# First FFN and preparation of a batch handed out a unit later in layer 0 of a two-layer macaron transformer

## The chip, the cores and the metric

The kernel runs on one core of one Trainium2 chip. The metric is the device time of one execution in microseconds, lower is better. The kernel before takes 3639.21 us, the median of 3 runs (3634.64 to 3644.63).

## The reference

The input x has 16 batches of 512 tokens with 128 channels. Two layers follow each other; the change lies in layer 0 alone. Cut to what matters:

```python
# layer 0
x = x + 0.5 * L0_ffn(layernorm(x))      # first FFN
x = x + L0_attn(layernorm(x))           # 16 heads of 8, clipped relative positions in scores and context
x = x + 0.5 * L0_ffn(layernorm(x))      # second FFN, same weights
# layer 1
x = x + 0.5 * L1_ffn(x)                 # attention over the batch axis, layer norm, mixture of 8 experts
x = x + L1_attn(x)                      # causal linear attention, relu features
x = x + 0.5 * L1_ffn(x)

def L0_ffn(x):                          # inputs and weights quantized to FP4 and back, blocks of 16
    h = silu(q(x) @ q(w_gate).T) * (q(x) @ q(w_up).T)   # 128 -> 352
    return q(h) @ q(w_down).T                           # 352 -> 128
```

## The kernel before

**Units.** Layer 0 (`layer0`) works on half batches. Unit u = 2b + h is half h (256 query rows) of batch b, 32 units in all. Each unit has these steps, and each is a Python generator that yields after a few instructions:

- `head(b,h)`: the first FFN of a half batch (`FFN.half`): statistics of the layer norm on VectorE (L55, L56), quantization on VectorE and GpSimd (L70 to L81), transposes and matmuls on TensorE, and the addition into x (L140). It begins with `xload(b)`, which takes one of five buffers of the tile x and issues the load on SP's queue (L475).
- `prep(b)`: the preparation of a whole batch for attention (`Attn0.prep`): layer norm, transposes, the q and k projections (L286), a split into two float16 parts (L143, L307), and 22 DMA stores on SP's queue to scratch tensors in DRAM: QM (L300), QS and KSd (L302), and rows of QS (L309). `prepV` makes the values.
- `loads(u)`: the loads of that scratch data on SP's queue: the keys KS (L315, once per batch), the queries BD (L329) and TQ (L330). BD and TQ have three buffers, KS two.
- `mxs(b,half)`: the row maxima of the scores. TensorE makes 32 score tiles (L263, and L267 near the diagonal) in three PSUM banks, VectorE takes each one's maxima (L341), and their negatives go through a small DRAM tensor MD (L353) back into a row of BD (L355).
- `main`: the same 32 score tiles again, now with the maxima in BD; ScalarE exponentiates each (L369), TensorE multiplies by the values and the relative table (L272, L274), ScalarE copies out (L403, L412), and the relative part goes through DRAM (L406, L409).
- `fin`: normalizes the context, output projection, addition into x (L443).
- `tail(b,h)`: the second FFN of the half, with `FFN.half` again, and the store of the result (L486).

The two FFNs share one set of work buffers (pool fk, two of each), and nearly all small matmuls and transposes share two PSUM banks (tag mps).

**Order.** A prologue runs some steps one after the other; everything else is put into a list S as (generator, number of steps, from, to), with from and to in units, and `interleave` hands out the step with the smallest place next. So a step that is listed from 3.9 to 5.0 is traced in equal portions over that stretch. The maxima run as one stream over all units, 33 steps each, and `loads(u+1)` is called at the 17th step of the maxima of unit u. By these places the loads of unit v are called at v - 1.94 and its maxima begin at v - 1.42.

The order in which the steps are handed out is not the order on the engines: it gives each instruction its rank. A planner then simulates the kernel with costs of its own and lets each engine take, among the instructions that are ready, the one handed out first. On the chip every engine and SP's queue keep the order that came out of this.

**The lines around the change** are the prologue (three x loads, first FFNs of batches 0, 1 and 2, preparation of batches 0 and 1, the maxima of unit 0 and 14 steps of those of unit 1), the table W with the places, and the constants pl and hl, which tell how many batches ahead the preparation and the first FFN are listed.

Of the kernel before, what the change touches and what calls it, by code (L numbers as in the profile page):

```python
# [141 lines left out]
def f16split(nc, src, hi, lo, eng_lo):  # L142
    nc.vector.tensor_copy(hi,src)  # L143
    eng_lo.tensor_tensor(lo,src,hi,ALU.subtract)

class Attn0:

    def __init__(a, s, wk, pp, wqkv, bqkv, wout, bout, rek, rev):
# [27 lines left out]
        OFF=a.OFF=168  # L176
        W=EW+32
        ekt=wk.tile([8,129],F32,name="ekt")
        with nc.allow_non_contiguous_dma(reason="small"):
            nc.sync.dma_start(ekt,rek.rearrange("r d -> d r"))  # L180
        nc.vector.tensor_tensor(ekt[:,1:],ekt[:,1:],ekt[:,0:1].to_broadcast([8,128]),ALU.subtract)
        pad=wk.tile([8,W],F32,name="pad")
        lo=OFF+24-64
        nc.vector.memset(pad[:,0:lo+1],0.0)
        nc.vector.tensor_copy(pad[:,lo+1:lo+129],ekt[:,1:129])
        nc.vector.tensor_copy(pad[:,lo+129:],ekt[:,128:129].to_broadcast([8,W-lo-129]))
        ph=wk.tile([8,W],F16,name="ph"); pl=wk.tile([8,W],F16,name="pl")
        f16split(nc,pad,ph,pl,nc.vector)
        padk=dr.tile([24,W],F16,name="padk")
        nc.sync.dma_start(padk[0:8],ph); nc.sync.dma_start(padk[8:16],ph); nc.sync.dma_start(padk[16:24],pl)  # L190
# [255 lines left out]
def interleave(*gens):  # L446

    live=[[g,n,0,f,t] for g,n,f,t in (q if len(q)==4 else (*q,0,1) for q in gens)]
    while live:
        k=min(live,key=lambda r:r[3]+(r[4]-r[3])*r[2]/r[1])  # L450
        try: next(k[0]); k[2]+=1
        except StopIteration: live.remove(k)
# [4 lines left out]
def layer0(tc, s, w, src, dst, nb=16):  # L457
    nc=tc.nc
    tok=lambda x,b: x[b].rearrange("(t p) d -> p t d",p=128)
    P="L0_attn_"; names=["W_qkv","b_qkv","W_out","b_out","rel_emb_k","rel_emb_v"]  # L460
    with ExitStack() as c:
        s.const=c.enter_context(tc.tile_pool(name="c",bufs=1))
        pM=c.enter_context(tc.tile_pool(name="pM",bufs=2,space=PS))
        pF=c.enter_context(tc.tile_pool(name="pF",bufs=0,space=PS)) if 0 else pM
        pS=c.enter_context(tc.tile_pool(name="pS",bufs=3,space=PS))
        pX=pS
        pA=c.enter_context(tc.tile_pool(name="pA",bufs=1,space=PS))
        wk=c.enter_context(tc.tile_pool(name="wk",bufs=1))
        fk=c.enter_context(tc.tile_pool(name="fk",bufs=2))
        xk=c.enter_context(tc.tile_pool(name="xk",bufs=5))  # L470
        X={}
        def xload(b):
            if b in X or b>=nb: return
            t=xk.tile([128,4,128],F32,name="x"); X[b]=t
            nc.sync.dma_start(t,tok(src,b))  # L475
        def head(b,h):

            if b<nb: xload(b); yield from F.half(X[b],h,fk,pF)
        def prep(b):
            if b<nb: yield from A.prep(b,X[b],wk,pM)  # L480
        def prepV(b):
            if b<nb: yield from A.prepV(b,pM)
        def tail(b,h):
            if b<0: return
            yield from F.half(X[b],h,fk,pF)
            nc.sync.dma_start(tok(dst,b)[:,2*h:2*h+2,:],X[b][:,2*h:2*h+2,:])  # L486
        def mxs(b,half):
            if b>=nb: return
            yield from A.maxima(b,half,wk,pX,pM)
        def loads(u):  # L490
            if u<2*nb:
                if u%2==0: A.loadK(u//2)
                A.load(u//2,u%2)
        def stream():
            for u in range(1,2*nb):
                for k,_ in enumerate(mxs(u//2,u%2)):
                    if k==16: loads(u+1)
                    yield
        st=stream()
        def part(n):  # L500
            for _ in range(n):
                if next(st,0)==0: return
                yield
        pl,hl=2,3
        W=dict(part=0,V=(.6,.7),fin=(.45,.9),prep=(0,.7),tail=1.0,head=(-.1,1))
        with tc.tile_pool(name="wp",bufs=1) as wp:
            for b in range(3): xload(b)
            F=FFN(s,w["L0_ffn_w_gate"],w["L0_ffn_w_up"],w["L0_ffn_w_down"],wp,pF)
            ffn2=lambda f,b: interleave((f(b,0),21,0,.8),(f(b,1),21,.2,1))
            ffn2(head,0)  # L510
            A=Attn0(s,wp,pS,*[w[P+n] for n in names])
            def run(g):
                for _ in g: pass
            run(prep(0)); run(prepV(0)); loads(0); run(mxs(0,0))
            FFN1.pre(s,wp,[pA.tile([128,512],F32,name=f"av{z}") for z in range(2)]+[pA.tile([128,512],F32,name="rps")],w)
        big=c.enter_context(tc.tile_pool(name="big",bufs=3))
        loads(1); ffn2(head,1); run(prep(1)); run(part(14)); ffn2(head,2)
        S=[(part(99999),33*2*nb,W['part'],2*nb+W['part'])]
        for b in range(nb):
            for h in range(2):  # L520
                u=2*b+h
                def at(g,n,f,t): S.append((g,n,u+f,u+t))
                at(A.main(b,h,X,wk,big,pS,pA,pM),59,0,1)
                fn,tl=(W['fin'],W['tail']) if u<2*nb-2 else ((.3,.5),.6)
                at(A.fin(b,h,X,wk,pM),5,1+fn[0],1+fn[1])
                at(tail(b,h),21,1+fn[1]+.001,1+fn[1]+tl)
                if b+hl<nb: at(head(b+hl,h),21,*W['head'])
                if h==0 and b+pl<nb: at(prep(b+pl),11,*W['prep'])
                if h==1 and b+1<nb: at(prepV(b+1),1,*W['V'])
        interleave(*S)  # L530
# [479 lines left out]
def run_stages(ctx, tc, w, out):  # L1010
    s = K(ctx, tc)
    X2 = s.dram.tile([16, 512, 128], F32, name="X2")
    layer0(tc, s, w, w["L0_attn_x"], X2)
    layer1(tc, s, w, X2, out)
# [23 lines left out]
```

## Time and profile before

| | |
|---|---|
| median of 3 runs | 3639.21 us (3634.64 to 3644.63) |
| the profiled execution | 3633.94 us, its span 3632.2 us |
| mean granted TensorE clock of the profiled execution | 0.90 |
| TensorE matmuls busy | 2825.0 us (78%) |
| VectorE busy | 2444.9 us (67%) |
| ScalarE busy | 1693.8 us (47%) |
| GpSimd busy | 838.9 us (23%) |
| last store of layer 0's result issued (L486) | 2044.9 us |
| statistics of x waiting for its load (L55) | 45.5 us in 11 times |

All durations come from one execution recorded by the hardware profiler, counted from its first instruction. Engines: PE is TensorE, PEld its weight loads, DVE VectorE, ACT ScalarE, POOL GpSimd, SP SyncE, which only issues DMAs here; "SPq" is SP's queue. A row of the timeline has start, duration, engine, line and operation, the tile written and the tiles read, the number of instructions merged, and in brackets the idle time of the engine before it and what ended it. A row of the waits has who waited for whom, the sum in us, how many times, and the longest. A row of the windows has the stretch, its length, and busy time and instruction count of each engine, then the granted clock, the share of the DMA engines' time and GB/s.

### The profile page before, as it was taken

How to read it: one execution, taken by the hardware profiler on the slowest of the kernel's cores; microseconds unless marked ns; L12 is line 12 of the kernel's file. 1: busy time of each engine (PE TensorE's matmuls, PEld its weight loads, DVE VectorE, ACT ScalarE, POOL GpSimd, SP SyncE). 2: the span in 40 equal slices, each digit the busy share in tenths (PEclk: the TensorE clock that was granted, in tenths of full speed). 3: DMA queues.
4: the chain of work that ended last, by engine and by line, in shares of the span. 5: the costliest groups of instructions: out<-in, count | busy, mean ns of one | idle time of the engine just before them, and what ended most of it. 6: DMA issues, size and time to landing. Idle time of an engine off the chain costs nothing. (4 is left out here: it accounts for less than half of the span.)

```text
span 3632.2 us, 95259 instructions
## 1 busy us (share of the span) xinstructions
PE 2825.0 (78%) x40077; PEld 2032.3 (56%) x40077; DVE 2444.9 (67%) x6508; ACT 1693.8 (47%) x3391; POOL 838.9 (23%) x789
## 2 busy tenths in 40 slices
PE   5578989889898889888896388873788888878570
PEld 3357777667676677666775244431565555555230
DVE  5568788777887788877773467774546655655356
ACT  3145555545455454545554155533455454445242
POOL 4122222222222222222110222212112211111226
PEclk8799999999999999999998599886899989989785
DMA  3232222321223222222210111104312222121401
GB/s 105 54 91 71 57 53 59 81 63 52 65 65 77 64 50 58 76 74 62 53 33 19 32 33 36 36 33 123 90 54 73 59 63 56 36 62 36 126 17 46
DMA packets 290159, 217.23 MB, mean 60 GB/s; under 512 B 77402, under 2 KB 257476, under 8 KB 289604
## 3 DMA queue, kind: packets, MB, share of 16 engines
q1 hardware_dynamic: 284468, 207.72, 21.6%
q8 instruction: 315, 5.16, 0.6%
q10 hardware_dynamic: 5264, 3.43, 0.4%
q14 instruction: 112, 0.92, 0.1%
HBM read 110.28 MB, written 100.78 MB: 58 GB/s over the span
## 5 line engine op out<-in xcount | busy, mean ns | idle before, releaser
L341 DVE TRANSPOSE_TENSOR_REDUCE mx<-sps 128x16 f32<-128x512 f32 x1024 | 702.5, 701 | 261.7 <-PE sps L263 137.2
L263 PE MATMUL sps<-a_BD,a_KS 128*128 128x128 f16 x8192 | 736.4, 222 | 136.2 <-DVE mx L341 65.6
L369 ACT ACTIVATE PT<-sps 128x512 f32<-128x512 f32 x1024 | 576.4, 599 | 433.8 <-PE sps L267 238.1
L263 PEld LDWEIGHTS <-a_KS 128*128 128x128 f16 x8192 | 546.1, 98 | 296.4 <-issue 260.0
L59 POOL TENSOR_TENSOR ln_rs<-ln_ve,negh 128x4 f32<-128x4 f32 (+1 forms) x192 | 176.9, 930 | 855.1 <-DVE ln_ve L58 760.6
L267 PE MATMUL sps<-a_TQ,a_ET 128*128 128x64 f16 x7168 | 370.3, 195 | 0.0
L721 DVE SCALAR_TENSOR_TENSOR moe<-mps,oh,moe 128x128 f32<-128x128 f32 x896 | 289.8, 341 | 110.7 <-PE mps L719 96.5
L79 POOL TENSOR_TENSOR q_M<-q_y,q_M 128x704 f32<-128x704 f32 (+2 forms) x129 | 157.0, 1218 | 784.6 <-DVE q_y L78 658.6
L719 PE MATMUL mps<-f_W,T 128*128 128x512 f32 x512 | 297.1, 701 | 24.8 <-DVE moe L721 20.0
L267 PEld LDWEIGHTS <-a_ET 128*128 128x128 f16 x7168 | 311.2, 99 | 2.3 <-issue 1.9
L274 PE MATMUL av<-PT,a_V 128*32 128x256 f32 x3840 | 251.9, 387 | 0.0
L894 DVE TENSOR_TENSOR a_at<-pp,a_cm 128x1024 f32<-128x1024 f32 x128 | 154.3, 1214 | 79.6 <-PE pp L892 78.6
L892 PE MATMUL pp<-a_F 64*128 64x128 f32 x2048 | 169.8, 306 | 41.4 <-DVE a_at L894 30.2
L892 PEld LDWEIGHTS pp<-a_F 64*128 64x128 f32 x2048 | 143.3, 206 | 93.0 <-DVE a_at L894 36.9
L719 PEld LDWEIGHTS mps<-f_W,T 128*128 128x128 f32 x512 | 102.7, 222 | 125.0 <-issue 75.3
L274 PEld LDWEIGHTS av<-PT,a_V 128*32 128x32 f32 x3840 | 121.4, 111 | 68.7 <-issue 5.0
L874 ACT ACTIVATE a_F<-pp 128x1024 f32<-128x1024 f32 x128 | 127.0, 1025 | 46.8 <-PE pp L872 40.5
L62 ACT ACTIVATE xn<-xn,ln_mr,ln_rs 128x128 f32<-128x128 f32 x256 | 103.6, 481 | 95.5 <-DVE ln_mr L60 75.2
L274 PE MATMUL rps<-PT,a_TV 128*32 128x64 f32 x6912 | 134.5, 222 | 4.6 <-issue 4.4
L139 PE MATMUL mps<-wdT,hT 128*128 128x128 f32 (+1 forms) x768 | 126.9, 301 | 5.6 <-ACT hT L136 4.0
L673 ACT COPY f_PT<-St 32x512 f32<-32x512 f32 x128 | 78.7, 615 | 106.0 <-DVE St L672 99.9
L872 PE MATMUL pp<-a_QK,a_PK 128*128 128x512 f16 x256 | 82.7, 413 | 54.4 <-DMA a_QK<-a1d 26.6
(342 smaller groups left out, 5330.2 us busy)
## 6 DMA issues: line engine op xcount, KB each, us to landing
QM<-a_HM SPq DMA_DIRECT2D x180, 128.0 KB
a_TQ<-QM SPq DMA_DIRECT2D x120, 192.0 KB
RD<-RV SPq DMA_DIRECT2D x32, 512.0 KB
a_KS<-KSd SPq DMA_DIRECT2D x128, 96.0 KB
a_QK<-a1d SPq DMA_DIRECT2D x128, 96.0 KB
xn<-X SPq DMA_DIRECT2D x32, 256.0 KB
a1d<-a_hi SPq DMA_DIRECT2D x64, 128.0 KB
a_BD<-QS SPq DMA_DIRECT2D x128, 58.0 KB
```

The costliest lines, as they stand in the source:

```text
L59: nc.gpsimd.tensor_tensor(rs,ve,s.negh[:,:n],ALU.pow); yield
L79: nc.gpsimd.tensor_tensor(M[:P],y[:P],M[:P],ALU.subtract)
L263: nc.tensor.matmul(o4[:,g],KS[:,sd,g*512+kt*128:g*512+(kt+1)*128],BD[:,g,:,b*32:b*32+32].rearrange("p h (x j) -> p x h j",j=4),start=(g==0 ...
L267: nc.tensor.matmul(out[:,x*64:x*64+64],a.ET[:,w0:w0+128],TQ[:,:,b*32+4*x:b*32+4*x+4],start=False,stop=(x==7),skip_group_check=True)
L274: for p,q in mms[1:]: a.nc.tensor.matmul(*p,**q)
L341: with a.s.tc.high_priority(): r=nc.vector.tensor_reduce(mx[:,kt,:,bb],ps.rearrange("p (i c) -> p i c",c=32),axis=AX.X,op=ALU.max,apply_tr ...
L369: nc.scalar.activation(pt[:,:,bb*32:bb*32+32].rearrange("p h (x j) -> p x h j",j=4),ps.rearrange("p (x h j) -> p x h j",x=8,j=4),AF.Exp)
L719: nc.tensor.matmul(ps,yT[:,j*128:(j+1)*128],a.W[:,e2*4:e2*4+4,:],start=True,stop=True)
L721: nc.vector.scalar_tensor_tensor(moe[:,j,:],ps[:,e*128:(e+1)*128],oh[:,j,e2*4+e:e2*4+e+1],moe[:,j,:],ALU.mult,ALU.add)
L874: nc.scalar.activation(f,ps,AF.Relu)
L892: nc.tensor.matmul(ps[:,hh,bs],f[hh*64:hh*64+64,1,bs],f[hh*64:hh*64+64,0,bs],start=True,stop=True)
L894: nc.vector.tensor_tensor(k,ps.rearrange("p h (b q) -> p (h b) q",b=4),a.cm.unsqueeze(1).to_broadcast([128,8,128]),ALU.mult)
```

## The change

The first FFN of a batch is listed two batches ahead instead of three, at places about one unit before its unit (so 0.95 units later than now); the preparation is listed one unit later and over a stretch of 0.9 instead of 0.7 units. The first FFN of batch 2 leaves the prologue for the list, where places before zero are moved to zero, and an end before 0.5 to 0.5. The three x loads at the start stay.

```diff
-        pl,hl=2,3
-        W=dict(part=0,V=(.6,.7),fin=(.45,.9),prep=(0,.7),tail=1.0,head=(-.1,1))
+        pl,hl=2,2
+        W=dict(part=0,V=(.6,.7),fin=(.45,.9),prep=(1.0,1.9),tail=1.0,head=(-1.15,-.05))
...
-        loads(1); ffn2(head,1); run(prep(1)); run(part(14)); ffn2(head,2)
+        loads(1); ffn2(head,1); run(prep(1)); run(part(14))
         S=[(part(99999),33*2*nb,W['part'],2*nb+W['part'])]
         for b in range(nb):
             for h in range(2):
                 u=2*b+h
-                def at(g,n,f,t): S.append((g,n,u+f,u+t))
+                def at(g,n,f,t): S.append((g,n,max(u+f,0),max(u+t,.5)))
...
                 if b+hl<nb: at(head(b+hl,h),21,*W['head'])
                 if h==0 and b+pl<nb: at(prep(b+pl),11,*W['prep'])
```

## The prediction

> **What bounds the kernel now.** A unit u=2b+h is half a batch of layer 0: 32 score tiles exponentiated (L369) while the row maxima (L341) of a later unit are taken. Counting the L369 rows off in groups of 32 dates the units: unit 0 begins at 175.5 us, 1 at 237.4, 2 at 306.0, 4 at 422.3, 5 at 480.1, 6 at 538.4, 26 at 1692.4, 27 at 1749.1, 30 at 1896.5. Layer 1 begins after 2050 and is not touched. First the page for the whole, then the sums of four stretches: the first two units, the steady ones 5 to 25, unit 26, and units 27 to 29, which have neither a first FFN nor a preparation.
>
> ```profile
> span 3632.2 us, 95259 instructions
> ...
> PE 2825.0 (78%) x40077; PEld 2032.3 (56%) x40077; DVE 2444.9 (67%) x6508; ACT 1693.8 (47%) x3391; POOL 838.9 (23%) x789
> ```
> ```profile
> core 0: us, PE busy (x) PEld busy (x) DVE busy (x) ACT busy (x) POOL busy (x), PEclk, DMA share, GB/s
> 175.50:306.00 130.50, 107.50 (x1816) 82.74 (x1814) 89.47 (x192) 60.28 (x133) 26.93 (x23) 0.92 0.30 76
> 480.10:1692.40 1212.30, 1075.45 (x19183) 850.75 (x19183) 966.33 (x2175) 617.08 (x1367) 289.46 (x271) 0.98 0.25 63
> 1692.40:1749.10 56.70, 48.96 (x871) 37.24 (x869) 38.85 (x79) 28.34 (x60) 11.62 (x11) 0.94 0.37 94
> 1749.10:1896.50 147.40, 132.65 (x2666) 108.30 (x2665) 106.27 (x213) 75.33 (x159) 15.34 (x15) 0.99 0.16 38
> ```
>
> In the steady stretch a unit takes 1212.3/21 = 57.7 us, with PE busy 89% and DVE 80%: PE sets the pace, and only its idle 6.5 us per unit can be won. So I asked what DVE, which frees PE's score banks, waits for there (units 5 to 25):
>
> ```profile
> DVE mx L341 <- PE sps L263: 87.9, 68, 3.0
> DVE mx L341 <- PE sps L267: 71.1, 86, 2.8
> DVE ln_st L55 <- DMA x<-in_L_attn_x_dram: 41.1, 10, 5.2
> ```
>
> The first two are DVE waiting for PE, many short ones. The third is the odd one: once per batch the layer-norm statistics of a new x wait for its load (45.5 us in 11 times over the whole run). The timeline around one of them, SP's queue, then DVE, then PE:
>
> ```profile
> 408.83 0.39 SPq L486 DMA_DIRECT2D X<-x  x1
> 412.11 0.40 SPq L475 DMA_DIRECT2D x<-in_L_attn_x_dram  x1
> ```
> ```profile
> 410.87 0.25 DVE L140 SCALAR_TENSOR_TENSOR x<-mps,x 128x128 f32<-128x128 f32 x1
> 415.46 1.06 DVE L55 BATCH_NORM_STATS2 ln_st<-x 128x6 f32<-128x128 f32 x5 [4.33 <-DMA x<-in_L_attn_x_dram]
> ```
> ```profile
> 418.07 0.58 PE L263 MATMUL sps<-a_BD,a_KS 128*128 128x128 f16 x4 [3.07 <-DVE mx L341]
> ```
>
> x has five buffers. The load of batch 5 needs batch 0's, so it waits for the store of its last half (issued 408.83), goes at 412.11, and its statistics start at 415.46. DVE stands 4.33 us, the score banks fill, and PE stands 3.07 us. This is what the change is aimed at.
>
> **The change, part by part.** Times are in units. The first FFN of half h of batch B is handed out from 2B+h-6.1 to 2B+h-5 now, and from 2B+h-5.15 to 2B+h-4.05 after: 0.95 later. The preparation moves from 2B-4..2B-3.3 to 2B-3..2B-2.1. No instruction is added or removed.
>
> *Price of the work that moves.* Unit 26 has a whole preparation and no first FFN, unit 28, also even, neither: 56.7 - 50.7 = 6.0 us; against the mean of 27 to 29 (147.4/3 = 49.1) 7.6. A steady unit has one FFN half and half a preparation more than those: 57.7 - 49.1 = 8.6. So an FFN half costs 8.6 - 3.0 or 8.6 - 3.8, about 5 us.
>
> *Start.* By the results' writes (L140) batch 2's first FFN ends at 208 to 229 us, inside unit 0, and before 175.5 only its input quantization runs, two times some 2.2 us on DVE. So it is hardly in the prologue now; taking it out frees at most 4.4 us, and I take 2. Units 0 and 1 now hold four FFN halves (batches 2 and 3), after it three: -5 us. They take 130.5 us, 15 over two steady ones, and one stop stands out, in the preparation of batch 2:
>
> ```profile
> 238.28 7.68 SPq L329 DMA_DIRECT2D a_BD<-QS  x4
> 246.08 3.32 SPq L302 DMA_DIRECT2D QS<-qkhi  x2
> ```
> ```profile
> 253.19 0.68 DVE L307 CAST qkhi<-mps 32x512 f16<-32x512 f32 x1 [8.43 <-DMA QS<-qkhi]
> ```
>
> L307 needs the buffer that the QS stores read, and those stand in SP's queue behind four BD loads; PE stands 9.0 us. After the change this preparation comes later, where SP is now idle (267 to 284 us), but another load may stand there. Between 0 and -9 I take -4. Start in all: -11.
>
> *End.* The last FFN half moves into unit 26, the last preparation from 26 to 27: one half more in the light units, +5 (to +7.6, if it weighs like a preparation). This gives back the start's -5.
>
> *The wait for x.* It costs PE some 3 us each of 11 times, 33 us: the ceiling. After the change the load can still go only when batch 0's store has landed, at the same moment; but its FFN is handed out near 4.85 instead of 3.9, and 0.95 units are 55 us against the load's 3.35. If the statistics stood at their new place the wait would be gone. Two things speak against that. The planner pulls ready work forward: the last two of the seven statistics at 415 to 417 are of half 1, handed out a whole unit later. And it keeps a tag's buffers in the order of the code: batch 4's x was loaded at 21 us, half 0's statistics ran at 60.4, half 1's only at 295, directly with the first second FFN, which the code names before them. For this change that order is good: now the second FFN of batch 1, ready since 400.4 (L443), stands in line behind the late x; after, batch 4's half stands there, its x long loaded. But batch 5's statistics are next, and may be pulled forward to the landing again. Between 0 and -33 I take half, -16.
>
> By the Trainium skill (DMA: Bandwidth & Descriptors, Anatomy of one DMA, SWDGE path) a transfer costs about 2.0 us and its bytes at 436 GB/s, so store and load would take an estimated 4.9 us, not the 6.6 of the rows; the term would shrink to about -9 and the sum to -15. The rows decide.
>
> The Trainium skill (TensorE: Matmul & The Clock Gate, Why this matters for your kernels) holds that PE gaps over some 3 us drop the clock; the gap here is 3.07 us, the granted clock of the stretch 0.98. By the rule each wait would cost an estimated 1.7 us more and the sum would be near -31; by the clock in the row nothing is added.
>
> *The preparation a unit later.* Its 22 DMA issues (12 QM, 3 QS, 3 KSd, and four of L309) take some 15 us of SP's time, now in even units (443 to 469), after in odd ones. There SP has room:
>
> ```profile
> 485.74 3.42 SPq L329 DMA_DIRECT2D a_BD<-QS  x2
> 515.45 1.31 SPq L353 DMA_DIRECT2D MD<-mn  x2
> ```
>
> Batch 4's FFN ends at 420 now and its first store goes at 443.7, 24 us later; a unit on that is 475 + 24 = 499, the last about 524. Its readers are the loads of unit 8: KS from 516.9, BD and TQ from 530.7 to 546, for maxima that start at 572.2. So some 23 us of slack remain: I cost it at nothing, and if that cover is gone, each us later is a us per batch, over 13 batches.
>
> Sum: -11 + 5 - 16 = -22 us. The profiled execution took 3633.9 us (span 3632.2), 5.3 below the median of 3639.2; the difference is put on the median: 3617.
>
> **The rivals.**
>
> *The wait stays.* The planner pulls batch 5's statistics to the planned landing, DVE meets them as early as now: -11 + 5 = -6, 3633 us. For: half 1's statistics are pulled a unit ahead today. Against: at their lower rank every ready maximum goes first, and the other FFN half fills DVE's gaps before.
>
> *Wholly gone.* -33, stop at 253 gone (-9), prologue -4.4, half -5, end +4: -47, 3592 us.
>
> *Slower: the preparation's stores get in the way of MD.* The maxima's result goes out at 515.45, comes back into BD by 524 and some 2.5 us of landing, and main of unit 6 starts at 538.4: 12 us of slack. My reckoned stores (499 to 524) cover 515. If all 15 us stand ahead of MD, the main of each even unit starts 3 us late: 13 x 3 = 39, with the rest -22 + 39 = +17, 3656 us. It decides once MD goes more than 12 us later in the odd unit than now. Against: the planner orders SP by readiness.
>
> **How the numbers follow.** The forecast has 0.46, the wait that stays 0.22, wholly gone 0.10, the late MD 0.22. 0.3% (11 us) is about what a measurement of this kernel can tell from no change. Faster: 0.40 + 0.10 + 0.04 = 0.54. Same: 0.05 + 0.13 + 0.02 = 0.20. Slower: 0.01 + 0.05 + 0.20 = 0.26. The range reaches from below 3592 to above 3656, 3585 to 3665; the likeliest case's own is 3600 to 3628.
>
> **What would show it.** Right: L55's wait for x under 25 us in all; units 0 and 1 under 122 us together, no stop at L307; steady units at 57 or less; units 26 and 27 some 5 us longer in sum. Wrong: L55 still near 45 us (the second case); a long wait of PE for MD's BD row at the start of even units, with MD's issue late in SP's queue (the slower one); or BD and TQ loads that end after the previous maxima do, which would mean that the preparation's slack was misread.

## The result, and the profile after

The changed kernel took 3934.14 us (median of 4 runs, 3928.20 to 3939.69) where the kernel before took 3636.93 (4 runs, 3626.03 to 3644.63): ratio 1.0819, 95% interval 1.0787 to 1.0852. It is about 297 us slower; the forecast was 22 us faster. The profiled execution took 3934.47 us. Layer 0's first 26 units hold nearly all of it: unit 26 now begins at 1990.4 us, 298 later than before, and what follows takes 3 us longer.

The page of the changed kernel, first the whole, then the costliest line that had cost little before:

```profile
span 3932.8 us, 95181 instructions
...
PE 2891.8 (74%) x40077; PEld 2091.6 (53%) x40077; DVE 2508.0 (64%) x6508; ACT 1700.1 (43%) x3391; POOL 863.1 (22%) x789
...
L55 DVE BATCH_NORM_STATS2 ln_st<-x 128x6 f32<-128x128 f32 x192 | 47.4, 276 | 212.3 <-DMA x<-in_L_attn_x_dram 210.6
```

The same count of matmuls, all engines less busy in share: time went into standing still. L55, the statistics of a new x, waits 210.6 us for the load where it waited 45.5, again 11 times, now 16 to 21 us each.

The same stretches as before (units 0 and 1, units 5 to 25, unit 26, units 27 to 29); columns as in the prediction:

```profile
176.30:306.10 129.80, 107.42 (x1803) 83.82 (x1802) 84.79 (x178) 60.16 (x129) 26.92 (x23) 0.89 0.32 77
502.30:1990.40 1488.10, 1130.47 (x19167) 896.26 (x19164) 1019.11 (x2167) 624.29 (x1365) 311.61 (x273) 0.88 0.22 52
1990.40:2046.20 55.80, 49.83 (x893) 40.60 (x894) 44.74 (x94) 28.91 (x64) 12.27 (x10) 0.94 0.20 49
2046.20:2196.90 150.70, 136.01 (x2674) 109.91 (x2673) 109.20 (x218) 77.30 (x162) 19.39 (x18) 0.99 0.23 54
```

A steady unit takes 1488.1/21 = 70.9 us on average, against 57.7. It is not even: by the exponentials' rows, even units take 78 to 82 us and odd ones 61 to 65. The fourth row has no first FFN; it is 3 us longer than before, and the last preparation, which stood in unit 26, now stands in it. The granted clock of the steady stretch fell from 0.98 to 0.88, and PE's busy time there rose from 1075.45 to 1130.47 us for nearly the same number of matmuls: with the stops, the work between them got slower as well.

What VectorE waits for in units 5 to 25, the same view as before:

```profile
DVE ln_st L55 <- DMA x<-in_L_attn_x_dram: 191.0, 10, 21.2
DVE mx L341 <- PE sps L267: 69.8, 77, 2.3
...
DVE qkhi L307 <- DMA QS<-qkhi: 35.6, 8, 5.9
```

The timeline around the stop that the prediction showed (batch 5's x, which takes batch 0's buffer): SP's queue, then VectorE, then TensorE.

```profile
419.64 0.54 SPq L406 DMA_DIRECT2D RD<-RV  x1
420.22 0.45 SPq L329 DMA_DIRECT2D a_BD<-QS  x1
420.78 5.95 SPq L486 DMA_DIRECT2D X<-x  x1
426.77 3.93 SPq L329 DMA_DIRECT2D a_BD<-QS  x2
430.74 2.67 SPq L330 DMA_DIRECT2D a_TQ<-QM  x1
433.51 2.94 SPq L409 DMA_DIRECT2D a_cr<-RD  x4
436.50 0.57 SPq L329 DMA_DIRECT2D a_BD<-QS  x1
437.11 2.36 SPq L330 DMA_DIRECT2D a_TQ<-QM  x1
439.51 0.73 SPq L475 DMA_DIRECT2D x<-in_L_attn_x_dram  x1
```
```profile
417.95 0.27 DVE L140 SCALAR_TENSOR_TENSOR x<-mps,x 128x128 f32<-128x128 f32 x1
...
445.38 0.49 DVE L55 BATCH_NORM_STATS2 ln_st<-x 128x6 f32<-128x128 f32 x2 [19.60 <-DMA x<-in_L_attn_x_dram]
```
```profile
446.61 1.01 PE L263 MATMUL sps<-a_BD,a_KS 128*128 128x128 f16 x8 [18.21 <-DVE ln_mv L56]
```

The last result (L140) that the store of batch 0 waited for in the kernel before:

```profile
407.30 0.29 DVE L140 SCALAR_TENSOR_TENSOR x<-mps,x 128x128 f32<-128x128 f32 x1
```

(The L140 row at 410.87 in the prediction begins after this store was issued, so it belongs to another FFN.) Unit 4 begins at nearly the same time in both kernels (422.3 before, 421.6 after). Before, the last result comes at 407.30, the store is issued at 408.83, and the load follows 3.3 us later. Now the last result comes at 417.95. Most of this is the preparation, which stands in this unit too: where it alone is moved (`prep_alone_later`, below) the result comes 5.5 us ahead of unit 4, against 15.0 before and 3.7 here. So the store moves out of the stretch where SP only loads keys, into the one where it sends the relative part to DRAM (RD) and loads BD and TQ, and the load is issued 18.7 us after the store. VectorE has reached the statistics at 425.8 and stands 19.6 us; TensorE, with all score banks full, 18.2.

### The profile page after: what moved, and what is told of

Read it like the earlier page. It is cut to its first block, busy times and chain, and to the rows that moved or that the text cites. A ratio compares the mean times of both kernels' runs of the same rounds, so it can differ in the third digit from the quotient of the medians.

```text
span 3932.8 us, 95181 instructions
## 1 busy us (share of the span) xinstructions
PE 2891.8 (74%) x40077; PEld 2091.6 (53%) x40077; DVE 2508.0 (64%) x6508; ACT 1700.1 (43%) x3391; POOL 863.1 (22%) x789
## 5 line engine op out<-in xcount | busy, mean ns | idle before, releaser
L263 PE MATMUL sps<-a_BD,a_KS 128*128 128x128 f16 x8192 | 768.4, 227 | 344.9 <-DVE ln_mv L56 158.5
L263 PEld LDWEIGHTS <-a_KS 128*128 128x128 f16 x8192 | 568.8, 101 | 538.6 <-issue 502.6
L341 DVE TRANSPOSE_TENSOR_REDUCE mx<-sps 128x16 f32<-128x512 f32 x1024 | 701.8, 701 | 183.4 <-PE sps L267 131.9
L267 PE MATMUL sps<-a_TQ,a_ET 128*128 128x64 f16 x7168 | 376.0, 196 | 1.6 <-issue 1.4
L267 PEld LDWEIGHTS <-a_ET 128*128 128x128 f16 x7168 | 316.6, 100 | 4.1 <-issue 3.8
L55 DVE BATCH_NORM_STATS2 ln_st<-x 128x6 f32<-128x128 f32 x192 | 47.4, 276 | 212.3 <-DMA x<-in_L_attn_x_dram 210.6
L121 PE MATMUL mps<-wguT,f_x 128*128 128x352 f32 x256 | 119.7, 563 | 18.7 <-ACT f_x L116 17.5
```

What stands on the lines that cost most here:

```text
L263: nc.tensor.matmul(o4[:,g],KS[:,sd,g*512+kt*128:g*512+(kt+1)*128],BD[:,g,:,b*32:b*32+32].rearrange("p h (x j) -> p x h j",j=4),start=(g==0 ...
L267: nc.tensor.matmul(out[:,x*64:x*64+64],a.ET[:,w0:w0+128],TQ[:,:,b*32+4*x:b*32+4*x+4],start=False,stop=(x==7),skip_group_check=True)
L341: with a.s.tc.high_priority(): r=nc.vector.tensor_reduce(mx[:,kt,:,bb],ps.rearrange("p (i c) -> p i c",c=32),axis=AX.X,op=ALU.max,apply_tr ...
```

## The experiments

Two theories. **The queue and the rank**: x's load goes late, because its place on SP's queue is behind BD, TQ and RD, and VectorE has the statistics in front of ready work. **The preparation** ("theory W" at first, "theory C" later): its place among the odd unit's maxima, its stops at L307 and its 22 DMA issues make the units long, and the wait for x only shows it. Ratios are against the kernel before, run on the same chip each time; 1% is some 36 us. In the kernels with a pin the lines after L50 have numbers one higher than in the text (L55 is L56, L307 is L308).

**1. The load's place.** `load_rank_back` lists the load alone where it was before the change:

```diff
+        def xl(b):
+            xload(b); yield
...
+                if h==0 and 5<=b+3<nb: S.append((xl(b+3),1,u-.05,u))
```

> The changed kernel, with the x loads of batches 5 to 15 handed out again where they were before (place 2B-6.05), the first FFN and the preparation staying a unit later. Theory Q (queue): the changed kernel loses its time because the x load stands on SP's queue behind loads that cost the planner little and the chip much: in the changed trace the store goes at 420.8 us, then BD, TQ, the RD copy, BD, TQ, and the x load only at 439.5, while DVE stands 19.6 us. With its old rank the load passes only the last part of these (three of the RD copies, one BD and one TQ, some 5 to 6 us), so the waits of L55 fall from 210 us to about 150 and the time from 3934 to about 3870. Theory W (work): the time is lost because the preparation's work and stores now fall into the odd units; the load's rank matters little: 3910 to 3940.

Measured: 3914.28 us, ratio 1.0732 (1.0695 to 1.0770). The load still comes 13.5 to 17.0 us after the store, and L55 waits 196.1 us. The time lies in the range of theory W, and theory Q's was missed. The load's rank is not what holds it: by the time that the store is issued the burst of RD, BD and TQ transfers is there.

`x_load_on_pool_queue` takes it off SP's queue:

```diff
-            nc.sync.dma_start(t,tok(src,b))
+            (nc.gpsimd if b>4 else nc.sync).dma_start(t,tok(src,b))
```

> The changed kernel, with the x loads of batches 5 to 15 issued on GpSimd's queue instead of SP's; everything else is handed out as in the changed kernel. Theory Q: the load no longer stands behind BD, TQ and RD, only behind its own buffer's store: L55 waits 40 to 90 us in all instead of 210 and the time falls to 3660 to 3740. Theory W: DVE's wait for x is only where a lateness shows that has its cause elsewhere; the time stays over 3850 and other waits take its place.

Measured: 3874.66 us, ratio 1.0619 (1.0582 to 1.0656), L55's wait 159.4 us. The expectation of the queue theory was missed by over 130 us; the time lies where theory W put it, but other waits did not take the place of L55's: the time fell with it. The rows tell why:

```profile
424.40 5.83 SPq L486 DMA_DIRECT2D X<-x  x1
```
```profile
434.86 0.97 POOL L475 DMA_DIRECT2D x<-in_L_attn_x_dram  x1 [8.72 <-DMA X<-x]
```

Nothing stands before the load on this queue but the landing of the store, and that alone takes 9 to 13 us from the start of the store's row, among the other transfers (2.2 to 3.9 us before the change). The row itself, which was 0.4 to 1.0 us long before, is 1.4 to 8.7 us of this. From the load's issue to the statistics it is another 6 to 8 us (3.35 before). The Trainium skill (DMA: Bandwidth & Descriptors, Issuing engines are not separate DMA queues) says that transfers issued by different engines run on the same DMA engines and interleave, so that another issuer saves issue time only. This run agrees: of the 297 us it gave back some 70.

**2. The statistics' rank.** `statistics_pinned` leaves the late load as it is, and lets the statistics of a first FFN be issued only after the last row maximum handed out:

```diff
-            nc.vector.bn_stats(st[:,j,:],xb[:,j,:])
+            last=pin() if pin else None
+            with s.tc.issue_after(last) if last is not None else nullcontext(): nc.vector.bn_stats(st[:,j,:],xb[:,j,:])
...
-            if b<nb: xload(b); yield from F.half(X[b],h,fk,pF)
+            if b<nb: xload(b); yield from F.half(X[b],h,fk,pF,(lambda: A.last) if b>4 else None)
```

> The changed kernel, with the first FFN's statistics (L55, from batch 5 on) kept behind the last maximum handed out before them, so that the planner can't pull them forward to the landing of x. The x load keeps its late place on SP's queue. Theory Q: the load is harmful only because DVE's order has the statistics right at the planned landing; pinned, they stand up to a unit after it: L55 waits under 30 us in all, the time is 3600 to 3660. Theory W: over 3850, as the preparation's place is not touched.

Measured: 3698.50 us, ratio 1.0143 (1.0106 to 1.0180). The load still goes 9 to 21 us after the store, and nobody waits for it:

```profile
L56 DVE BATCH_NORM_STATS2 ln_st<-x 128x6 f32<-128x128 f32 x192 | 45.5, 267 | 0.7
```

Some 0.068 of the 0.082 is gone, while the load still goes late; the time is 38 us above theory Q's range and far below W's. Most of the loss is not the late load but an instruction that waits for it in front of ready work.

The same by a second way, without touching the order: `after_other_x` normalizes the x tile of the batch before, loaded long ago.

```diff
-        yield from s.ln_steps(xh,xn,wk,2)
+        yield from s.ln_steps(xh if ob is None else ob[:,2*half:2*half+2,:],xn,wk,2)
...
-            if b<nb: xload(b); yield from F.half(X[b],h,fk,pF)
+            if b<nb: xload(b); yield from F.half(X[b],h,fk,pF,X[b-1] if b>4 else None)
```

> The changed kernel, with the layer norm of the first FFN from batch 5 on reading the x tile of the batch before, as in prep_alone_other_x; not pinned, L307 as in the changed kernel. If the wait for x is what costs some 236 us, and the pin of statistics_pinned won by taking it away: 3685 to 3715 us. If the pin won by the order that it forces on VectorE: 3760 to 3900 us.

Measured: 3723.03 us, ratio 1.0222 (1.0183 to 1.0261): 8 us above the range of the first case, far below the second. The wait for x is worth 0.060 of the 0.082 by this way. L307 waits more here (57 us for the QS and KSd stores from 480 to 1680 us, 44 in `statistics_pinned`).

**3. What is left: L307.** This line writes 32x512 results into the buffers that the QS and KSd stores read. In the changed kernel these stores stand on SP's queue behind the row-maximum store MD and its reading back into BD, and VectorE waits for them; SP's queue, then VectorE:

```profile
539.42 1.31 SPq L353 DMA_DIRECT2D MD<-mn  x2
...
544.92 2.45 SPq L355 DMA_DIRECT2D a_BD<-MD  x4
...
548.02 0.60 SPq L302 DMA_DIRECT2D QS<-qklo  x1
548.67 0.60 SPq L302 DMA_DIRECT2D QS<-qkhi  x1
```
```profile
551.90 0.68 DVE L307 CAST qkhi<-mps 32x512 f16<-32x512 f32 x1 [5.00 <-DMA QS<-qkhi]
```

`pinned_own_rows` adds to `statistics_pinned` that L307 writes into a tag that no QS or KSd store of L302 reads. It is the preparation's own tag xn (not one of the first FFN, as the expectation says), and its earlier contents are read by L144 on GpSimd:

```diff
-        rhi=wk.tile([128,512],F16,name="qkhi",bufs=2)[:32]; rlo=wk.tile([128,512],F16,name="qklo")[:32]
+        r16=wk.tile([128,4,128],F32,name="xn").rearrange("p a b -> p (a b)").bitcast(F16); rhi=r16[:32,0:512]; rlo=r16[:32,512:1024]
```

> The statistics_pinned kernel (the changed kernel with the first FFN's layer-norm statistics issued after the last row maximum handed out), and L307's 32x512 results no longer written into the tag that the QS and KSd stores read, but into a tag of the first FFN that is free there. Nothing else is moved. Theory R (the some 50 us that statistics_pinned still stands above the kernel before are L307's stops for the QS and KSd stores, some 5 us in 7 to 10 batches each, 82 us by the waits of the changed kernel's steady stretch at most): 3640 to 3670 us, no wait of L307 over 1 us in the steady stretch. Theory O (the 50 us come from the order itself: the preparation stands among the odd unit's maxima and its 22 DMA issues stand ahead of the row-maximum store MD): the stops at L307 are only replaced by waits further on (L353, L341), 3690 to 3705 us, odd units still over 61 us.

Measured: 3646.74 us, ratio 1.0015 (1.0000 to 1.0030); as theory R had it: L307's waits for the stores are gone, and it stands 20 us in all, where it stood 76 in `statistics_pinned`. With both stops taken away and every step at the change's place, nothing that matters is left of the loss, and nothing is won. Here too the load goes late: batch 5's is issued 17.4 us after the store.

`after_own_rows` has the last diff alone on the changed kernel:

> The changed kernel, its statistics not pinned, with only L307's stop taken away. Theory S: VectorE meets the pulled-forward statistics earlier and waits for x that much longer; 3910 to 3960 us, L55's wait above its 211 us. If the two stops add up instead: 52 us less, 3870 to 3895 us, L55's wait as now.

Measured: 3942.68 us, ratio 1.0811 (1.0784 to 1.0838), the same as the changed kernel, L55's wait up from 211 to 237 us. The numbers are those of theory S, but the run does not test it, because L307 still stops. It now waits for L144 on GpSimd, which reads xn and itself waits for the store of qklo (143 us in 15 times); the waits from 480 to 1680 us:

```profile
DVE xn L307 <- POOL qklo L144: 42.0, 8, 6.9
```

L307 stands 77 us in all, against 91 in the changed kernel. So it stays open what L307's stop is worth while the wait for x is there; the 0.013 is known only from `statistics_pinned` to `pinned_own_rows`.

**4. The preparation alone.** `prep_alone_later` is the kernel before with one number pair changed, and the first FFN where it was:

```diff
-        W=dict(part=0,V=(.6,.7),fin=(.45,.9),prep=(0,.7),tail=1.0,head=(-.1,1))
+        W=dict(part=0,V=(.6,.7),fin=(.45,.9),prep=(1.0,1.9),tail=1.0,head=(-.1,1))
```

> The kernel before with the preparation alone handed out a unit later (1.0 to 1.9); first FFNs, prologue and x loads stay. Theory Q: the later preparation pushes its readers, the KS, BD and TQ loads, into the time of the tail's store and the x load, but here the x load keeps a rank ahead of most of them: L55 waits 70 to 120 us in all, the time 3660 to 3740. Theory W: most of the loss is the preparation's place, so 3850 to 3940.

Measured: 3723.47 us, ratio 1.0203 (1.0163 to 1.0243): a step that the sum had at nothing costs 74 us. The time is in theory Q's range, though L55 waits 64 us in all and not 70 to 120. The waits from 480 to 1680 us:

```profile
DVE ln_st L55 <- DMA x<-in_L_attn_x_dram: 55.6, 10, 6.5
DVE qkhi L307 <- DMA QS<-qkhi: 44.4, 10, 6.4
DVE qklo L307 <- DMA KSd<-qklo: 18.6, 10, 2.8
```

In this kernel the load still follows the store by 3.0 to 4.5 us; its statistics wait longer than before all the same. More runs try to take the stops away. `prep_alone_own_rows` (L307's):

> prep_alone_later (the kernel before with the preparation placed 1.0 to 1.9 units after its old window's start instead of 0 to 0.7), with L307 writing to a tag that no store reads. prep_alone_later stood at 1.0203 of before, some 74 us; the waits there were L307's (63 us in the steady stretch) and x's (56 us, against 41 before). If L307's stops are the cost of the later preparation: 3640 to 3675 us. If the row-maximum store and the x load behind the preparation's 22 DMA issues are: 3700 to 3730 us, with L307's wait gone and no shorter units.

Measured: 3739.46 us, ratio 1.0272 (1.0241 to 1.0304). L307's wait for the stores is gone and the kernel is slower: L55's wait for x grew from 64.4 to 113.5 us. Both cases of the expectation missed. As in `after_own_rows`, L307 still stops, for GpSimd: 68 us in all, against 90.

`prep_alone_pinned` and `prep_alone_pinned_own_rows` (the pin's diff, and both):

> prep_alone_later with the first FFN's statistics issued after the last row maximum handed out. Theory S (the stop for x and L307's stop are the whole cost of the later preparation and stand in for each other): the wait for x goes, L307's stays or grows, 3680 to 3710 us, as statistics_pinned. Theory C (the later preparation costs by itself, through its place among the odd unit's maxima or its DMA issues): 3700 to 3730 us.

> prep_alone_pinned, and L307 writing to a tag that no store reads: both stops taken away. Theory S: nothing of the cost is left, 3625 to 3655 us. Theory C: 3670 to 3720 us.

Measured: 3780.20 us, ratio 1.0363 (1.0342 to 1.0385), and 3737.46 us, ratio 1.0249 (1.0226 to 1.0272). By their numbers these speak for theory C, 50 and 17 us above its ranges, but they did not test it: L55 still waited 99 us for x in both, and in the second L307 still stood 44 us for GpSimd. Here the first FFN is handed out so early that its statistics wait for x even behind the maxima, and the pin does not help.

`prep_alone_other_x` takes that wait away by other data, as in `after_other_x`, with L307 on its own tag:

> prep_alone_own_rows (the preparation later, L307 writing to a tag that no store reads), and the layer norm of the first FFN from batch 5 on reads the x tile of the batch before, loaded long ago, in place of its own; it leaves out the normalization of the batch's own x, all else stays, its own x is still loaded and is added at the end of the FFN (L140). Theory S (the stop for x and L307's stop are the whole cost of the later preparation): 3620 to 3655 us. Theory C (it costs by its place, whatever the stops): 3680 to 3730 us.

Measured: 3603.51 us, ratio 0.9894 (0.9862 to 0.9927), below the range of theory S. The steady stretch, in one row:

```profile
480.00:1680.00 1200.00, 1078.43 (x19313) 852.86 (x19311) 961.82 (x2166) 617.25 (x1369) 283.59 (x273) 0.98 0.27 66
```

L307 stands 67 us for GpSimd here too, so from `prep_alone_own_rows` to this run only the wait for x was taken away, and with it went 0.038 of the time. The preparation's later place, with its 22 issues around MD, shows no cost once that wait is gone, and the preparation theory falls, except for what L307's waits for the stores cost. `before_other_x` has the same data in the kernel before (with L307 as it was):

> The kernel before with the same substitution: its wait for x goes, all placements stay. If before_pinned's 3628 us is what the wait for x is worth there: 3620 to 3636 us. If TensorE's 33 us are to be won and the pin gave part of them back: 3600 to 3615 us.

Measured: 3622.41 us, ratio 0.9940 (0.9920 to 0.9960), in the first of the two ranges. In these kernels the statistics are also free to go earlier than any x could allow, and L307's waits for the stores grew here (from 5 to 44 us between 480 and 1680 us), so their gain is not what an earlier load of the right x would bring.

**5. The prologue's part.** `pinned_prologue_ffn` is `pinned_own_rows` with the third batch's first FFN back in the prologue:

```diff
-        loads(1); ffn2(head,1); run(prep(1)); run(part(14))
+        loads(1); ffn2(head,1); run(prep(1)); run(part(14)); ffn2(head,2)
...
-                if b+hl<nb: at(head(b+hl,h),21,*W['head'])
+                if 3<=b+hl<nb: at(head(b+hl,h),21,*W['head'])
```

> pinned_own_rows (the change without its two stops), with the third batch's first FFN back in the prologue, as in the kernel before. This prices the prologue's part of the change by itself. By the prediction's terms (2 us in the prologue, one FFN half of 5 us out of units 0 and 1): 7 us above pinned_own_rows, 3650 to 3658 us. If that work only fills idle time in units 0 and 1 (the units that the trace shows 15 us longer than steady ones whatever stands in them): within 3 us of pinned_own_rows. If its absence from the prologue delays the batch: below pinned_own_rows.

Measured: 3655.94 us, ratio 1.0035 (1.0018 to 1.0052) beside 1.0015 (1.0000 to 1.0030). The sizes fit the 7 us expected, but the intervals overlap, and the profiles point the other way (units 0 and 1 took 122.7 us with it, 126.2 without). It stays undecided, and is small either way.

**6. What the wait in the kernel before was worth.** `before_pinned` and `before_pinned_own_rows` are the kernel before with the pin, and with both edits; all places as before.

> The kernel before, with the first FFN's layer-norm statistics issued after the last row maximum handed out; placements, tags and loads as before. This asks what the wait that the change was aimed at is worth: 45.5 us on VectorE in 11 times, some 33 us on TensorE. Theory V (VectorE standing for x is time lost at the end): 3605 to 3620 us. Theory N (the wait only takes the place of waits of VectorE for other work that come anyway): within 12 us of the kernel before, with L55's wait for x gone and the waits for TensorE's scores or ScalarE's products longer by as much.

> before_pinned, and L307 writing to a tag that no store reads (as in pinned_own_rows); x in one tile, unlike before_halves_pinned. L307 waits only some 5 us in the steady stretch of the kernel before and 8.4 us once in unit 1. If the stop in unit 1 is on the path: 5 to 9 us below before_pinned. If not: within 4 us of it. If the half tiles were what cost before_halves_pinned its gain: 10 us or more below its 3632 us.

Measured: 3628.46 us, ratio 0.9970 (0.9952 to 0.9989), and 3627.60 us, ratio 0.9965 (0.9950 to 0.9980). Both are some 12 us faster than the kernel before. Theory N holds by its number, just: of L55's 41 us of waits (480 to 1680 us) 5 are left, and others have grown, shown for `before_pinned`:

```profile
DVE qkhi L144 <- ACT qk L292: 40.4, 10, 5.1
DVE f_h L124 <- ACT f_h L123: 34.2, 20, 2.1
```

Before, these two stood at 16.5 and 8.3 us in about the same stretch: together 50 us more on VectorE, for 36 won at L55 and 24 at the maxima (L341, for L267: 68 before, 44 here). L307's single 8 us stop in unit 1 is not on the path (0.0005 between the two runs).

Three runs had x as two half tiles, each half loaded when its half of the FFN is handed out:

```diff
-            t=xk.tile([128,4,128],F32,name="x"); X[b]=t
-            nc.sync.dma_start(t,tok(src,b))
+            t=X[b].t[h]=xk.tile([128,2,128],F32,name=f"x{h}")
+            nc.sync.dma_start(t,tok(src,b)[:,2*h:2*h+2,:])
```

> The kernel before, with x as two half tiles, each loaded by itself when its half of the first FFN is handed out; placements as before. The wait for x of the kernel before is 45.5 us on VectorE in 11 times, at most some 33 us on TensorE. Theory L (the wait is the load's stand behind the store of the very last half: a half loaded earlier ends it): the first half's statistics no longer wait, 3605 to 3635 us. Theory Q (where on SyncE's queue a load stands decides, and a half load that is put behind four strided BD and TQ loads waits again, as in the changed kernel): the second half's load comes late, 3650 to 3720 us.

Measured: 3918.14 us, ratio 1.0756 (1.0733 to 1.0779), theory Q beyond its range: L55 waits 284 us. The half's store goes at 433.86 us, then four KS, four BD and four TQ issues, and the load at 451.46. It is the changed kernel's fault, a late load with its reader in front of ready work, made in the kernel before with all places of the table as they were; here it is the load's own place on the queue that makes it late.

> The kernel before with its own placements, x as two half tiles, the statistics pinned behind the last row maximum, and L307 writing to the free tag: the three stops that the runs have shown, taken away without moving any step to another unit. If TensorE's gaps at the two stops are all that there is to win: 33 us for x and up to 20 for L307, so 3590 to 3625 us. If the stops only make room for the next wait (maxima that wait for TensorE's scores): 3625 to 3645 us.

> pinned_own_rows, and x as two half tiles of 2x128 rows each, so that each half is loaded by itself into the room that the half stored a unit earlier has left. This asks whether the load that still lands 9 to 21 us after the store costs anything once the statistics no longer stand and wait for it. If the pin alone has taken its cost away: within 10 us of pinned_own_rows. If the late load still holds up the first FFN of the batch: 15 to 40 us below pinned_own_rows.

Measured: 3632.44 us, ratio 0.9973 (0.9956 to 0.9991), and 3665.23 us, ratio 1.0059 (1.0040 to 1.0079). With the pin and L307's own tag the half tiles are harmless in the one and cost 19 us in the other, which neither case of its expectation had; they win nothing.

## Why the prediction was wrong

**The step that failed** is the wait for x: "After the change the load can still go only when batch 0's store has landed, at the same moment". The load did have to wait for the landing, but the moment was another. The store did not keep its time: its data come from the second FFN of batch 0 on VectorE, and with the preparation moved into that unit the last L140 came 10.6 us later. And neither the landing nor the load followed the store as closely: I had counted the preparation's 22 issues as a load on SP's queue, but had not followed where the X store and the x load come to stand. Before, they lay among KS loads; after, among RD, BD and TQ. Moving the preparation alone does not do this: in `prep_alone_later` they still lie among KS and BD loads, the store ahead of RD. It takes the first FFN's move as well, and no run moves that alone. So the term, bounded between 0 and -33 us, was some +217 to +246 (0.060 and 0.068 of 3637, from `after_other_x` and `statistics_pinned`). A loss was not among its bounds at all.

**The warning was in the text.** "The planner pulls ready work forward", and the statistics "may be pulled forward to the landing again", was right in its mechanism; `statistics_pinned` shows what the rank alone is worth. That the planner counted on an earlier landing than the chip's is inferred from the rows; no run measured its plan. The rival "the wait stays" left this wait at what it was, though nothing in the trace held it to that: it is the difference of two moments, and I had moved both. The 4.9 us that the prediction set beside the rows for store and load (the Trainium skill, DMA: Bandwidth & Descriptors, Anatomy of one DMA, SWDGE path) go by a formula for transfers that GpSimd issues, which these are not; from the store's issue to the statistics the rows have 6.6 us before and 24.6 after.

**The ceiling** of 33 us for the wait was not reached by any way of taking it from the kernel before: without any wait for x it wins 0.4 to 0.8% (`before_other_x`), 15 to 29 us, and with a pin, 4 to 17. In both, other waits of VectorE grew.

**The preparation at nothing** was wrong as the kernel stands: +74 us alone. It was right once the wait for x is away and L307 does not wait for the stores: no cost in `prep_alone_other_x`. The maxima of its batch did not wait for it, as reckoned: in the changed kernel the loads of unit 8 are issued by 579.6 us and its maxima begin at 620.1. What I did not look at was who waits for the stores' buffers, although L307's stop at 253.19 us was in front of me: I weighed it in the start alone, not once per batch. Its rival ("the preparation's stores get in the way of MD") had the two the wrong way round: from unit 4 on, MD is issued at most 1.9 us after its data are ready, and it is the stores that stand behind it. It was priced at 39 us; L307's part is 0.013, some 47.

**The start**, -11, did not come: unit 2 begins at 306.1 us against 306.0, and units 0 and 1 took 129.8 us against 130.5. L307's 8.4 us stop shrank to 3.6, but the same stretch now has a wait of 8.8 us of the maxima for TensorE (VectorE's waits, last column the longest):

```profile
DVE mx L341 <- PE sps L267: 21.3, 13, 8.8
```

**The end**, +5, held in size: units 26 and 27 took 110.9 us against 105.3.

**The clock.** The rule that I weighed and set aside (the Trainium skill, TensorE: Matmul & The Clock Gate, Why this matters for your kernels: gaps of TensorE over some 3 us drop the clock) fits the runs. At 3 us of gap the granted clock was 0.98; with gaps near 18 us once per batch it is 0.88, 0.90 to 0.97 in the runs between, and 0.98 again in `prep_alone_other_x`. In the steady stretch the lower clock went with 1130.47 - 1075.45 = 55 us more of busy time, a part of the loss that no list of waits shows.

**What stays open**: the prologue's part (under 10 us); what the first FFN's move does alone; why `prep_alone_own_rows` is slower than `prep_alone_later`; and whether a kernel with the right x could have the 36 us of `prep_alone_other_x`.

## What to carry to other kernels

When a step moves, follow the moved work's neighbours: for each load that waits for a buffer, write down the whole chain (last writer, store, landing, load) with what stands before each link on its queue, after the change as well as before. In a kernel with a fixed order per engine the cost of a late load is set by the rank of its first reader: the same late load took the kernel to 1.08 where its reader stood in front of ready work, and to 1.0015 where it stood behind it and L307's stop was away as well. A stop that is taken away may give little back, because the engine then waits elsewhere (36 us less at L55 in `before_pinned`, 12 us of time), so a suspect is priced by the time, and by a second way. And look in the trace whether an edit that is to remove a stop removed it: L307's new tag only gave it another to wait for.

## What was not expected of the hardware

A 128 KB store from 128 partitions (X) landed within 2.2 to 3.9 us among a few loads, and took 9 to 13 us among BD, TQ and RD transfers, although the DMA engines' mean share in the steady stretch was only 0.23 (`x_load_on_pool_queue`). The order on SP's queue goes with it. In the kernel before, `prep_alone_later` and `prep_alone_other_x` the X store is issued ahead of the 512 KB store RD, and all 33 loads are issued 2.2 to 4.5 us after it. In the changed kernel, `load_rank_back` and `x_load_on_pool_queue` it is issued 1.0 to 1.9 us after RD, and all 33 come 9 to 21 us after it. No run moved RD alone.
